# A graph network on one core: ranks and looked-up scores as maxima read from PSUM, bfloat16 masks widened by ScalarE, edge sums added in the rows' scatter

## The chip, the cores and the metric

The kernel runs on one core of one Trainium2 chip. The metric is the time of one execution on the device in microseconds (us), taken as the median over runs. Engines are called as the profile calls them: PE (TensorE matmul), PEld (its weight loads), DVE (VectorE), ACT (ScalarE), POOL (GpSimd), SP (SyncE, which issues most DMAs).

## The reference, cut to what matters

There are N = 6250 nodes with 128 features, and E = 100,000 edges sorted by their end `dst`, each with a start `src`, a weight and 128 attributes. Two graph convolutions with self-loops come first, then an attention layer over edges:

```python
h = gcn_conv(x, src, dst, ew, W1, b1)        # out[dst] += (x @ W)[src] * norm
h = gcn_conv(relu(h), src, dst, ew, W2, b2)
x = layernorm(x + sigmoid(h))
...
z, rh = x @ fc_w.T, edge_attr @ fc_r_w.T
e = leaky_relu(z[src] @ aw[0] + z[dst] @ aw[1] + rh @ aw[2])
alpha = softmax of e over the edges of one dst
agg = segment_sum(alpha[:, None] * (z[src] + rh), dst)
out = layernorm(x + relu(agg + z @ loop_w))
```

## The kernel before, in words

**Tiles.** Nodes lie in 49 blocks of 128. Edges are worked on in 49 chunks of 2048 (`NC`, `CC`), as 128 partitions by 16 (`TC`) or as 16 rows of 128 (`NL`). As the edges are sorted by `dst`, all ends of a chunk fall into a window of 144 nodes (`WC`). The sums over `dst` lie transposed in SBUF (features by nodes): `acc1`, `acc2`, and `sum_r` for the attributes.

**Slots.** Before conv1 can take rows by `src`, the edges of each chunk are sorted into slots by the block of their `src`: 12 groups (`GP`) of four blocks with 32 slots each hold "near" edges, 5 groups (`GS`) hold the rest, "far" edges. The sort is a plan of small steps, worked off beside conv1. For each chunk `count` builds a one-hot of the blocks, `oh`; `add_up` (L750 to L763) counts with matmuls into PSUM how many edges of the same block stand ahead of each place, and ACT casts that to `own` (L763); `take` (L766 to L774) multiplies `own` by `oh` on DVE (L769), folds it in three additions (L773) and reduces it to one rank per edge (L774). Later steps spread the edges' records (ACT `rec`, L818; DVE `put`, L266 and L825), gather them into slots by matmul (L834) and keep slot numbers (L842 to L847): `sdst` (the place in the window), `swt` (the weight), `sidx` (the far rows).

**One chunk of a convolution.** `pick` (L495) gets the rows. The near ones come from the table `hot` in SBUF (three bfloat16 parts that add up to float32) by 144 one-hot matmuls (L507) into PSUM, copied and scaled by ACT into `got` (L512). The far ones come from DRAM by five indirect DMAs on POOL (L516). Then DVE builds the float32 masks `wm`: 12 near ones of 144 columns in one instruction (L522), five far ones of 64 in another (L529). `weigh` (L546) lets ACT scale the far masks by their weights. `scatter` (L549) adds the chunk up with 17 float32 matmuls in PSUM (L553, each shows as two records), and `add_in` (L556) adds the window to `acc1` or `acc2` on DVE (L558). `scatter` of a chunk stands after `pick` of the next.

**Stages.** conv1 and conv2 run in the order in which the code is written (`manual_schedule`); conv3 and the tables are put in order by a planner. In conv1, `steps_now` says how many sort steps go beside each chunk. conv2 also computes, on DVE, the products of the edge attributes with the attention weights (`dots_of`, L938 and L939), and turns the `src` numbers of all edges into places with 16 transposes (`blks`). In conv3, for each half chunk, `starts` (L1249) looks up the score of each edge's `src`: a broadcast row of places `rk` is compared with the partition number (L1255), ACT doubles the block numbers (`blk2`, L1258), DVE builds the one-hot `ohb` of 8 by 50 (L260 in `equal_to`), 24 matmuls (L1263) give for each edge the scores at its place in all 49 blocks, and DVE multiplies by `ohb` (L1266, `sel`) and adds up (L1267). The PSUM pool of these has one buffer. After softmax, `edge_part` (L1385 to L1425) sums the weighted attributes: masks `mb` and `ms` (L1402, DVE), 32 matmuls (L1413), an ACT copy `sw` (L1418), two more matmuls (L1424) and `add_in` to `sum_r`. `out_of` (L450) multiplies `sum_r` by the attribute weights (L461), adds `sum_x` (L462), and a norm and a store end the work. The look-ups of later edge batches go beside the sums of earlier ones (`beside`), so the first 33 chunks of conv3 have them and the last 14 don't.

Every line number is that of the kernel before.

Of the kernel before, what the change touches and what calls it, by code (L numbers as in the profile page):

```python
# [19 lines left out]
P = 128  # L20
# [15 lines left out]
NOWHERE = 99.0  # L36


@with_exitstack
def gnn_kernel(ctx, tc, x, src, dst, ea, ew, W1, b1, W2, b2, fcw, fcrw, attn, loopw, out):  # L40
# [78 lines left out]
    srd = dram.tile([NC, GP * P], BF16, name="srd")  # L119
    drow = dram.tile([NC, P], BF16, name="drow")  # L120
# [12 lines left out]
    nc.vector.tensor_copy(iotab, iota_i)  # L133

# [16 lines left out]
    iotap, iotaq = iotap2[:, 0:1], iotap2[:, 1:2]  # L151

    trib = const.tile([P, P], BF16, name="trib")
    nc.vector.tensor_scalar(trib, iota[:, :P], iotap, None, op0=OP.is_gt)

# [36 lines left out]
    sdst = keep.tile([P, NC, G], BF16, name="sdst")  # L192
# [13 lines left out]
    blks = keep.tile([P, NC, NL], BF16, name="blks")  # L206
# [49 lines left out]
    def equal_to(out, of, n):  # L256

        row = iotab[:, :n].rearrange("p (h d) -> p h d", d=2)
        some = [P, of.shape[1], n // 2, 2]
        nc.vector.tensor_tensor(out.rearrange("p t (h d) -> p t h d", d=2), row[:, None].to_broadcast(some),  # L260
                                of[:, :, None, :].to_broadcast(some), op=OP.is_equal)
# [190 lines left out]
    def out_of(sum_x, sum_r, b0, n, xp, pool, tag):  # L452
# [6 lines left out]
        for b, nb in some:  # L459
            of = slice(b * P, b * P + nb)  # L460
            nc.tensor.matmul(agg[:nb, b - b0, :], sum_r[:, of], wfrT, start=True, stop=False)  # L461
            nc.tensor.matmul(agg[:nb, b - b0, :], sum_x[:, of], ident, start=False, stop=True)  # L462
# [35 lines left out]
    def pick(c, mask, hot, table, ps_g, wp, gots=4, fars=12):  # L498
# [15 lines left out]
        for g in range(GS):  # L514
# [5 lines left out]
        wm = wp.tile([P, GP * WC + FARS], F32, name="wm")  # L520
        parts_, at = [], 0
        nc.vector.tensor_tensor(wm[:, : GP * WC].rearrange("p (g w) -> p g w", w=WC),  # L522
                                iota[:, None, 1 : WC + 1].to_broadcast([P, GP, WC]),
                                sdst[:, c, :GP, None].to_broadcast([P, GP, WC]), op=OP.is_equal)
        for g in range(GP):
            parts_.append((0, wm[:, g * WC : g * WC + WC]))
        at = GP * WC
        if c < CF:
            nc.vector.tensor_tensor(wm[:, at:].rearrange("p (g w) -> p g w", w=FW), fiota,  # L529
                                    sdst[:, c, GP:, None].to_broadcast([P, GS, FW]), op=OP.is_equal)  # L530
        for g, (n0, w) in enumerate(far_parts[c]):
            m = wm[:, at : at + w]
            if c >= CF:
                nc.vector.tensor_tensor(m, iota[:, 1 + n0 : 1 + n0 + w],
                                        sdst[:, c, GP + g : GP + g + 1].to_broadcast([P, w]), op=OP.is_equal)
            parts_.append((n0, m))
            at += w
        wm = parts_
        return c, rows, wm

    def weigh(held):

        c, rows, wm = held
        for g in range(GP, G):
            m = wm[g][1]
            nc.scalar.activation(m, m, AF.Copy, scale=swt[:, c, g : g + 1])  # L546

    def scatter(held, ps_w):
        c, rows, wm = held  # L549
        ps = ps_w.tile([P, WC], F32, name="win")  # L550
        for g in range(G):
            n0, m = wm[g]
            nc.tensor.matmul(ps[:, n0 : n0 + m.shape[-1]], rows[g], m, start=g == 0, stop=g == G - 1)  # L553
# [7 lines left out]
    relc = ed.tile([P, NC, TC], F32, name="relc")  # L561
# [7 lines left out]
    with tc.tile_pool(name="prep", bufs=1) as prep, tc.tile_pool(name="ps_p", bufs=3, space=PSUM) as ps_mm, \  # L569
# [50 lines left out]
        nc.vector.tensor_copy(bb, bb_ps)  # L620

# [102 lines left out]
    def plan_batch(at, c0, n):  # L724
# [24 lines left out]
        def add_up(c):  # L749
# [3 lines left out]
            for h in range(2):  # L753
                ks = slice(h * HB, h * HB + HB)
                full = ps[:, h, : HB * TC].rearrange("p (k t) -> p k t", t=TC)
                nc.tensor.matmul(full, trib, oh[:, ks, :], start=True, stop=False)
# [5 lines left out]
            own = sp.tile([P, BP, TC], BF16, name="own", bufs=2)  # L762
            nc.scalar.copy(own.rearrange("p (h k) t -> p h (k t)", h=2), ps[:, :, : HB * TC])  # L763
            of["own", c] = own, oh

        def take(c):  # L766

            own, oh = of.pop(("own", c))
            nc.vector.tensor_mul(own, own, oh)  # L769
            k = BP  # L770
            while k % 2 == 0 and k > 6:
                k //= 2
                nc.vector.tensor_tensor(own[:, :k, :], own[:, :k, :], own[:, k : 2 * k, :], op=OP.add)  # L773
            nc.vector.tensor_reduce(of["r"][:, c - c0, :], own[:, :k, :].rearrange("p k t -> p t k"), AX.X, OP.add)  # L774

        def spill():
# [3 lines left out]
            nc.vector.tensor_scalar(o, of["r"], float(CAP), None, op0=OP.is_ge)  # L780
# [14 lines left out]
        def slots_of_edges():  # L795
# [9 lines left out]
            nc.vector.tensor_add(r_, r_, sub[:, some, :])  # L805
# [31 lines left out]
        def keep_slots():  # L837
# [5 lines left out]
            nc.vector.tensor_copy(sdst[:, some, :], field[:, :, 1])  # L843
# [35 lines left out]
    for c0, n in sorts:  # L879
        at = plan_batch(at if len(ends_at) != 1 else ends_at[0], c0, n)  # L880
# [90 lines left out]
    with tc.tile_pool(name="conv", bufs=2) as wp, tc.tile_pool(name="ps_g", bufs=3, space=PSUM) as ps_g, \  # L971
# [16 lines left out]
        pace = [float(done[0])]  # L988

        def steps_now(c):  # L990

            due = [(ends_at[b], max(c0 - 3 - c, 0)) for b, (c0, n) in enumerate(sorts) if ends_at[b] > pace[0]]
            pace[0] += max(((end - pace[0]) / (left + 1) for end, left in due), default=0)
            return min(int(pace[0] + 0.999), len(plan))

        held, win = None, None
        with tc.manual_schedule():
# [3 lines left out]
            for c in range(NC):  # L1001
                to = steps_now(c)
                if held is not None:
                    weigh(held)
                if win is not None:
                    add_in(acc1, c - 2, win)
                sort_to(done[0] + (to - done[0]) // 3)
                new = pick(c, mask, hot, g1, ps_g, wp, 6, 11)
# [10 lines left out]
            weigh(held)  # L1019
# [624 lines left out]
```

## Time and profile before

| | |
|---|---|
| median of 14 runs | 2257.41 us (2242.03 to 2285.51) |
| the profiled execution | 2253.38 us |
| its span, first to last instruction | 2251.3 us |
| granted TensorE clock, mean | 0.864 |
| busy: PE, PEld | 1741.4 us (77%), 1498.2 us (67%) |
| busy: DVE, ACT, POOL | 1566.3 us (70%), 996.3 us (44%), 1025.7 us (46%) |
| DMA | 306.92 MB, mean 136 GB/s |

Busy time is the time in which an engine executes; matmuls are pipelined, so a busy PE is not one at its peak. In the rows of groups, the line and engine come first, then the operation with its output and inputs, the shapes, the count after x, the total busy us and the mean ns of one, and last the engine's idle time just before these instructions with what ended it. The stages of the span, in us: preparation, degrees and the first table to 213; conv1 with the sorting to 706; the rest of conv1 to 806; the second table to 892; conv2 to 1396; the start of conv3 to 1525; conv3 with look-ups to 2047, without to 2231; the last output.

### The profile page before, as it was taken

To read this page: it belongs to the slowest core of one execution; us is meant where nothing else is said; L and a number is where in the kernel's file an instruction comes from. 1 tells how busy PE (TensorE), PEld (TensorE's weight loads), DVE (VectorE), ACT (ScalarE), POOL (GpSimd) and SP (SyncE) were. 2 spreads that over 40 slices of the span, in tenths; PEclk is the share of its full clock that TensorE was granted. 3 is DMA by queue.
4 is the path that set the end of the run, shared out by engine and by line. 5 is a ranking of instruction groups with operands and counts; after the bars stand their busy time and mean duration, and the time that the engine had idled before them with its cause. 6 is when DMAs were issued, how large, how long until landed. Compare 5 with 4: busy or idle time off the path is not lost.

```text
span 2251.3 us, 79000 instructions
## 1 busy us (share of the span) xinstructions
PE 1741.4 (77%) x33767; PEld 1498.2 (67%) x33767; DVE 1566.3 (70%) x3222; ACT 996.3 (44%) x3341; POOL 1025.7 (46%) x952
## 2 busy tenths in 40 slices
PE   2866778887788887788888887468888888888886
PEld 2545666676677765677676776357777777777775
DVE  6777766776666768866766766687777676776553
ACT  1253434443344554556565665224343343434443
POOL 4033334443335746756666764213344333434552
PEclk9886878888889975988899898568899898989998
DMA  2122222323224765665655656554656456565562
GB/s 51 38 78 68 79 81 76 92 82 89 74 78 118 249 188 165 185 165 170 192 168 174 197 171 198 166 142 125 176 152 178 135 156 170 151 167 139 147 160 62
DMA packets 261376, 306.92 MB, mean 136 GB/s; under 512 B 38387, under 2 KB 193785, under 8 KB 260212
## 3 DMA queue, kind: packets, MB, share of 16 engines
q1 hardware_dynamic: 229311, 244.90, 35.5%
q0 software_dynamic: 23520, 48.22, 10.1%
q10 hardware_dynamic: 8184, 8.65, 1.3%
q8 instruction: 268, 4.39, 0.8%
q14 instruction: 93, 0.76, 0.1%
HBM read 260.42 MB, written 41.25 MB: 134 GB/s over the span
## 4 chain that ended last, share of the span: by engine, by line
PE 64%; issue 13%; DVE 11%; ACT 5%; DMA 4%; another core or an unknown queue 3%; SPq 0%; DVEq 0%; POOL 0%; ACTq 0%; POOLq 0%
PE win L553 25%; PE g L507 20%; PE r L1413 3%; PE k L1263 2%; PE rec L834 2%; PE mm L357 2%; PE rec L1424 2%; PE r L760 1%; ACT got L512 1%; DMA rk<-srow 1%; DVE sel L1266 1%; DVE put L266 1%; PE rec L1381 1%; DVE ohm L260 1%
## 5 line engine op out<-in xcount | busy, mean ns | idle before, releaser
L516 POOL DMA_INDIRECT far<-g,sidx x490 | 640.0, 1306 | 521.4 <-PE win L553 395.7
L507 PE MATMUL g<-hot,mask 128*32 128x128 bf16 x21168 | 557.0, 245 | 260.6 <-issue 237.6
L512 ACT ACTIVATE got<-g,swt 128x128 f32<-128x128 f32 x1764 | 490.8, 377 | 476.7 <-PE g L507 235.0
L507 PEld LDWEIGHTS <-mask 128*32 128x32 bf16 x21168 | 415.1, 109 | 381.0 <-issue 355.3
L516 POOL DMA_INDIRECT far<-zd,sidx x245 | 318.3, 1299 | 506.5 <-PE win L553 410.5
L553 PE MATMUL win<-wm,got 128*128 128x144 f32 x3528 | 517.7, 306 | 6.4 <-issue 4.3
L553 PEld LDWEIGHTS win<-wm,got 128*128 128x128 f32 x3528 | 489.4, 206 | 24.5 <-issue 16.0
L522 DVE TENSOR_TENSOR wm<-iota,sdst 128x1728 f32<-128x1728 f32 x147 | 286.8, 1951 | 2.0 <-PE g L507 2.0
L546 ACT ACTIVATE wm<-wm,swt 128x64 f32<-128x64 f32 (+1 forms) x735 | 196.5, 350 | 73.8 <-DVE swt L1382 47.8
L553 PE MATMUL win<-wm,far 128*128 128x64 f32 (+1 forms) x1470 | 180.7, 269 | 2.4 <-DMA far<-g,sidx 2.3
L553 PEld LDWEIGHTS win<-wm,far 128*128 128x128 f32 x1470 | 177.9, 192 | 2.8 <-issue 2.7
L558 DVE TENSOR_TENSOR acc<-acc,win 128x144 f32 x147 | 44.5, 303 | 175.7 <-PE win L553 163.4
L1263 PE MATMUL k<-adp,rk 128*128 128x49 bf16 x2352 | 102.9, 195 | 56.2 <-DVE sel L1266 25.0
L1263 PEld LDWEIGHTS <-rk 128*128 128x128 bf16 x2352 | 87.5, 103 | 74.0 <-issue 56.3
L260 DVE TENSOR_TENSOR ohm<-iotab,pm 128x2048 bf16<-128x2048 bf16 x98 | 120.0, 1225 | 0.0
L346 POOL TENSOR_TENSOR hot<-low,hot 128x512 bf16<-128x512 f32 x24 | 38.6, 1607 | 133.8 <-DVE spilled L798 69.6
L266 DVE TENSOR_TENSOR put<-ohg,rec 128x1440 bf16<-128x1440 bf16 x49 | 45.6, 930 | 62.7 <-ACT rec L818 41.4
L763 ACT CAST own<-r 128x768 bf16<-128x768 f32 x49 | 39.5, 806 | 111.0 <-PE r L760 57.2
L1266 DVE TENSOR_TENSOR sel<-k,ohb 128x392 f32<-128x392 f32 x98 | 54.6, 557 | 47.2 <-remote 26.4
L939 DVE TENSOR_REDUCE dots<-et 128x12 f32<-128x1536 f32 (+1 forms) x49 | 85.9, 1753 | 1.6
L938 DVE TENSOR_TENSOR et<-et,ar_row 128x1536 f32<-128x1536 f32 (+1 forms) x49 | 85.5, 1745 | 0.0
L834 PE MATMUL rec<-put,ohm 128*128 128x95 bf16 x784 | 53.6, 233 | 27.7 <-DVE put L825 20.6
(401 smaller groups left out, 2275.6 us busy)
## 6 DMA issues: line engine op xcount, KB each, us to landing
et<-in_edge_attr_dram SPq DMA_DIRECT2D x97, 512.0 KB
mask<-masks SPq DMA_DIRECT2D x98, 384.0 KB
et<-in_edge_attr_dram SPq DMA_DIRECT2D x48, 768.0 KB
rk<-srow SPq DMA_DIRECT2D x98, 256.0 KB
mask<-srd SPq DMA_DIRECT2D x49, 384.0 KB
masks<-mask SPq DMA_DIRECT2D x49, 384.0 KB
ee<-in_edge_attr_dram SPq DMA_DIRECT2D x24, 512.0 KB
far<-g,sidx POOLq DMA_INDIRECT x490
```

Source lines behind the costliest of these rows:

```text
L260: nc.vector.tensor_tensor(out.rearrange("p t (h d) -> p t h d", d=2), row[:, None].to_broadcast(some), of[:, :, None, :].to_broadcast(some ...
L507: nc.tensor.matmul(ps[32 * q : 32 * q + 32, g, :], mask[:, (g0 + g) * P + 32 * q : (g0 + g) * P + 32 * q + 32], hot[:, 4 * (g0 + g) + q, k ...
L512: nc.scalar.activation(got[:, g, :], ps[:, g, :], AF.Copy, scale=swt[:, c, g0 + g : g0 + g + 1])
L516: nc.gpsimd.indirect_dma_start(out=got, out_offset=None, in_=table[:, :], in_offset=bass.IndirectOffsetOnAxis(ap=sidx[:, c, g : g + 1], ax ...
L522: nc.vector.tensor_tensor(wm[:, : GP * WC].rearrange("p (g w) -> p g w", w=WC), iota[:, None, 1 : WC + 1].to_broadcast([P, GP, WC]), sdst[ ...
L546: nc.scalar.activation(m, m, AF.Copy, scale=swt[:, c, g : g + 1])
L553: nc.tensor.matmul(ps[:, n0 : n0 + m.shape[-1]], rows[g], m, start=g == 0, stop=g == G - 1)
L834: nc.tensor.matmul(ps, ohm[:, t, :], put[:, t, :NF], start=t == 0, stop=t == TC - 1)
L938: nc.vector.tensor_mul(part, part, ar_row[:p, None, None, :].to_broadcast([p, *part.shape[1:]]))
L939: nc.vector.tensor_reduce(dots[:p, c : c + m, ts], part, AX.X, OP.add)
L1263: nc.tensor.matmul(ps[:, s, :], mk[:, s * P : (s + 1) * P], adp[:, 0, k, :NB], start=k == 0, stop=k == 2)
L1266: nc.vector.tensor_mul(sel, ps, ohb[:, :, :NB])
```

## The change

Five things are done at once.

1. *Ranks.* The triangular matrix of the counting matmul gets 4096 (`RB`) on its diagonal, so that an edge's own block holds the greatest of its 48 sums. `take` is one DVE maximum straight from PSUM; later thresholds and sums take 4096 off again. The cast, the product and the additions go.
2. *Looked-up scores.* A fourth matmul in each place adds `other`: 0 in the block of the edge and minus a great number in the other ones, from a second broadcast row `bk` of the block numbers, compared once a chunk. One DVE maximum from PSUM gives the score. `blk2`, `ohb` and `sel` go, and conv2's transposes into `blks` give way to a cast and a DMA to `bsrc`.
3. *Masks.* `sdst` is kept twice over, so that DVE compares bfloat16 pairs into `wb`; ACT copies the near masks to float32 in two halves, and scales the far ones to float32 as `weigh` did, now inside `pick`. conv2 keeps its near masks as they were (`halved=False`).
4. *Edge sums.* ACT copies the window of `edge_part` to `sr`, and the next `scatter` has it as an 18th matmul with the attribute weights. `sum_r`, its clearing on POOL, its `add_in` and L461 go. The product `ms` is made on POOL.
5. *Order.* The second batch of the sort may start four steps earlier, steps are paced in whole numbers, conv1 takes `pick` before `add_in`, masks are loaded two chunks ahead (three buffers), and the last output groups are worked off side by side.

```diff
+    iotar = const.tile([P, 1], F32, name="iotar")
+    nc.vector.tensor_scalar(iotar, iotap, 64.0, -64.0, op0=OP.is_ge, op1=OP.mult)
+    nc.vector.tensor_add(iotar, iotar, iotap)
+    other = const.tile([P, 2, NB], BF16, name="other")
+    for h in range(2):
+        nc.vector.tensor_scalar(other[:, h, :], iota[:, :NB], iotar, -BIG, op0=OP.not_equal, op1=OP.mult)
+        nc.vector.memset(other[64 - 64 * h : 128 - 64 * h, h, :], 0.0)
...
+    nc.vector.scalar_tensor_tensor(tribig, ident, RB, trib, op0=OP.mult, op1=OP.add)
...
-    sdst = keep.tile([P, NC, G], BF16, name="sdst")
+    sdst = keep.tile([P, NC, G, 2], BF16, name="sdst")
...
-            nc.tensor.matmul(agg[:nb, b - b0, :], sum_r[:, of], wfrT, start=True, stop=False)
-            nc.tensor.matmul(agg[:nb, b - b0, :], sum_x[:, of], ident, start=False, stop=True)
+            if sum_r is not None:
+                nc.tensor.matmul(agg[:nb, b - b0, :], sum_r[:, of], wfrT, start=True, stop=False)
+            nc.tensor.matmul(agg[:nb, b - b0, :], sum_x[:, of], ident, start=sum_r is None, stop=True)
...
-        wm = wp.tile([P, GP * WC + FARS], F32, name="wm")
+        wm = wp.tile([P, NEAR + FARS], F32, name="wm")
+        wb = wp.tile([P, NEAR * halved + FARS], BF16, name="wb", bufs=1)
+        if halved:
+            equal_to(wb[:, :NEAR].rearrange("p (g w) -> p g w", w=WC), sdst[:, c, :GP], WC, iota1)
+            half = GP // 2 * WC
+            for n0 in (0, half):
+                nc.scalar.copy(wm[:, n0 : n0 + half], wb[:, n0 : n0 + half])
+        else:
...
         for g, (n0, w) in enumerate(far_parts[c]):
...
+            nc.scalar.activation(m, b, AF.Copy, scale=swt[:, c, GP + g : GP + g + 1])
...
-    def weigh(held):
...
-                nc.tensor.matmul(full, trib, oh[:, ks, :], start=True, stop=False)
+                nc.tensor.matmul(full, tribig, oh[:, ks, :], start=True, stop=False)
...
-            own = sp.tile([P, BP, TC], BF16, name="own", bufs=2)
-            nc.scalar.copy(own.rearrange("p (h k) t -> p h (k t)", h=2), ps[:, :, : HB * TC])
...
-            nc.vector.tensor_mul(own, own, oh)
-            k = BP
-            while k % 2 == 0 and k > 6:
-                k //= 2
-                nc.vector.tensor_tensor(own[:, :k, :], own[:, :k, :], own[:, k : 2 * k, :], op=OP.add)
-            nc.vector.tensor_reduce(of["r"][:, c - c0, :], own[:, :k, :].rearrange("p k t -> p t k"), AX.X, OP.add)
+            nc.vector.tensor_reduce(of["r"][:, c - c0, :],
+                                    ps[:, :, : HB * TC].rearrange("p h (k t) -> p t h k", t=TC), AX.XY, OP.max)
...
-        at = plan_batch(at if len(ends_at) != 1 else ends_at[0], c0, n)
+        at = plan_batch(at, c0, n)
...
-                if held is not None:
-                    weigh(held)
+                sort_to(done[0] + (to - done[0]) // 3)
+                new = pick(c, mask, hot, g1, ps_g, wp, 6, 11)
                 if win is not None:
                     add_in(acc1, c - 2, win)
-                sort_to(done[0] + (to - done[0]) // 3)
-                new = pick(c, mask, hot, g1, ps_g, wp, 6, 11)
...
-            nc.vector.tensor_copy(d_f, s_j)
-            by_partition(ps_mm, lambda t, ps: nc.scalar.copy(blks[:, :, t], ps), lambda t: ds_[:, t, :])
+            nc.vector.tensor_copy(s_k, s_j)
+            nc.sync.dma_start(bsrc[:, :], s_k)
...
-    nc.gpsimd.memset(sum_r, 0.0)
...
+                if i % 2 == 0:
+                    bks[i // 2] = lp.tile([P, HC], BF16, name="bk", bufs=3)
+                    for h in range(2):
+                        nc.sync.dma_start(bks[i // 2][64 * h : 64 * h + 64, :],
+                                          bsrc[i // 2, None, h * HC : (h + 1) * HC].to_broadcast([64, HC]))
...
-                ohb = lp.tile([P, NL // 2, NBE], BF16, name="ohb")
-                blk2 = lp.tile([P, NL // 2, 2], BF16, name="blk2")
-                nc.scalar.copy(blk2, twice(blks[:, c, of]))
-                equal_to(ohb, blk2, NBE)
+                bk = bks[c]
+                if h == 0:
+                    nc.vector.tensor_scalar(bk, bk, iotar, None, op0=OP.is_equal)
...
+                    nc.tensor.matmul(ps[:, s, :], bk[:, s * P : (s + 1) * P], other[:, h, :], start=False, stop=True)
                 yield
-                sel = lp.tile([P, NL // 2, NB], F32, name="sel", bufs=1)
-                nc.vector.tensor_mul(sel, ps, ohb[:, :, :NB])
-                nc.vector.tensor_reduce(asr[:, 1 + c * NL + of.start : 1 + c * NL + of.stop], sel, AX.X, OP.add)
+                nc.vector.tensor_reduce(asr[:, 1 + c * NL + of.start : 1 + c * NL + of.stop], ps, AX.X, OP.max)
...
-            nc.vector.tensor_mul(ms, mb, aw[:, i, :, None].to_broadcast([P, NL, WS]))
+            nc.gpsimd.tensor_mul(ms, mb, aw[:, i, :, None].to_broadcast([P, NL, WS]))
...
-            return ps
+            sr = mp.tile([P, WC], F32, name="sr")
+            nc.scalar.copy(sr, ps)
+            return sr
...
-                    weigh(held)
                     win = scatter(held, ps_w)
-                ps = edge_part(c, aw, c - c0)
+                new[1].append(wfrT)
+                new[2].append((0, edge_part(c, aw, c - c0)))
...
-                add_in(sum_r, c, ps)
...
-        pieces.go(N, 999)
+        pieces.finish()
```

## The prediction

> **What bounds the kernel now.** I looked first at the clock of the one core (0.864 over the span), then at the chain that ended last, to see which engine sets the end.
>
> ```profile
> PE 64%; issue 13%; DVE 11%; ACT 5%; DMA 4%; another core or an unknown queue 3%; SPq 0%; DVEq 0%; POOL 0%; ACTq 0%; POOLq 0%
> ```
>
> TensorE (PE, with its issue time) is 77% of what ends last, VectorE (DVE) 11%. The change takes work mostly from DVE, so the 11% is the field in which it can win. Where it lies is read from a table of windows at the stage borders (start:end, length, busy us of PE, weight load, DVE, ACT, POOL, then clock, DMA share, GB/s):
>
> ```profile
> 213.00:706.00 493.00, 392.40 (x7257) 339.65 (x7255) 336.63 (x736) 202.75 (x708) 199.76 (x176) 0.84 0.29 82
> 706.00:806.00 100.00, 85.06 (x1988) 75.80 (x1984) 65.83 (x88) 57.61 (x206) 73.79 (x53) 0.95 0.69 211
> 892.00:1396.00 504.00, 418.90 (x8645) 365.20 (x8646) 351.44 (x442) 295.68 (x944) 331.64 (x235) 0.90 0.59 178
> 1396.00:1525.00 129.00, 72.20 (x1325) 59.93 (x1324) 95.52 (x278) 34.13 (x121) 23.43 (x17) 0.64 0.56 164
> 1525.00:2047.00 522.00, 431.78 (x9395) 383.35 (x9393) 393.68 (x969) 211.10 (x770) 205.52 (x161) 0.90 0.57 155
> 2047.00:2231.00 184.00, 150.23 (x3349) 132.38 (x3349) 97.26 (x212) 82.00 (x304) 94.80 (x69) 1.00 0.54 141
> ```
>
> They are: conv1 with the sorting, conv1's tail, conv2, the serial start of conv3, conv3 with looked-up scores (33 chunks, 15.8 us each), conv3 after them (14 chunks, about 13 us each). PE is the busiest in all but one. Only in 1396:1525 is DVE ahead (95.5 of 129 us, PE at 0.64 of its clock). In 1525:2047 DVE is near (393.7 against 431.8). Followed stage by stage, the chain gives DVE about 25 us of 493 in the first window, 43 of 129 in the fourth, 70 of 522 in the fifth: about 138 us in all. Then the rows that the change touches (form, count | busy us, mean ns | idle before and its releasers), and PE's waits in conv3 (us, times, longest):
>
> ```profile
> L522 DVE TENSOR_TENSOR wm<-iota,sdst 128x1728 f32<-128x1728 f32 x147 | 286.8, 1951 | 2.0 <-PE g L507 2.0
> L260 DVE TENSOR_TENSOR ohm<-iotab,pm 128x2048 bf16<-128x2048 bf16 x98 | 120.0, 1225 | 0.0
> L260 DVE TENSOR_TENSOR ohb<-iotab,blk 128x400 bf16<-128x400 bf16 x98 | 34.7, 355 | 0.0
> L1263 PE MATMUL k<-adp,rk 128*128 128x49 bf16 x2352 | 102.9, 195 | 56.2 <-DVE sel L1266 25.0 <-issue 20.9 <-DVE rk L1255 6.9
> L1266 DVE TENSOR_TENSOR sel<-k,ohb 128x392 f32<-128x392 f32 x98 | 54.6, 557 | 47.2 <-remote 26.4 <-PE k L1263 19.1 <-PE agg L462 1.0
> L1402 DVE TENSOR_TENSOR ms<-mb,aw 128x512 f32<-128x512 bf16 x49 | 33.4, 682 | 0.0
> L763 ACT CAST own<-r 128x768 bf16<-128x768 f32 x49 | 39.5, 806 | 111.0 <-PE r L760 57.2 <-issue 39.8 <-DVE rank L774 10.5
> L461 PE MATMUL agg<-wfrT,sum_r 128*128 128x128 f32 x96 | 22.0, 315 | 0.1
> ```
> ```profile
> PE k L1263 <- DVE sel L1266: 25.0, 22, 10.6
> PE rec L1424 <- ACT sw L1418: 21.1, 30, 1.8
> ```
>
> **The change, part by part**, on the profiled execution's own 2253.38 us (span 2251.3, 2.1 around it). That is 4.0 below the median of the 14 runs, 2257.41, so 4.0 goes on at the end.
>
> *1. Ranks.* Per chunk ACT's cast own (0.806) goes, and on DVE the product L769 (0.553), three additions L773 (0.357, 0.256, 0.206) and the reduce L774 (0.323): 1.695 us. In their place comes one maximum over 768 float32 from PSUM. No row has that; the nearest are L939 (1536 elements, 1.753; 1024, 1.213: 1.055 ns each) and L1267 (392, 0.552), which give 0.95. DVE saves 0.75 x 49 = 37 us, ACT 39.5. This lies beside PE work but for DVE's 25 of 493 us, and the ranks' waits (DVE own on ACT own, 40.6 us in 13 waits) are DVE's own idle time. The single PSUM buffer of the ranks is now freed by DVE, in whose order the maximum stands later than the cast did on ACT. I take **-5**, ends -12 and +5.
>
> *2. Looked-up scores.* PE gets 16 matmuls more per chunk (a fourth beside three), 784 in all. From the row L1263 they cost 44 ns each when busy (102.9/2352): **+34**. Ends: the fastest group of 24 took 0.77 us, 32 ns each, so +25; with the idle time of the row (159.1/2352 = 68 ns) +53. DVE loses sel (0.557) and ohb (0.355) of each half chunk and gains one bk comparison per chunk (as L1255, 0.50): -1.3 us a chunk. ACT loses 20 us of blk2. Off the chain comes what waited on sel, 25.0 us; of ohb's 34.7 busy us I count 23% (in the fourth and fifth windows 113 of DVE's 489 busy us were on the chain): -8. The 16 transposes taken out of conv2 are within 2 us. Two more DMAs a chunk go on SP's queue and, 128 KB each by their tile, are small beside 512 KB et loads; cover gone, the rk wait of 6.9 us shows their size. Sum **+1**, ends -20 and +33.
>
> *3. Masks.* By L260 (355 ns at 400, 1225 at 2048) 1728 bf16 elements in pairs take 1.06 us against 1.95, 320 take 0.31 against 0.48: DVE saves 1.06 us a chunk in conv1 and conv3, about 104 in all. ACT pays two copies of 864, 0.9 each by its slope between 512 (0.615) and 768 (0.806) plus start: 1.75 x 98 = 172 us. ACT is 41% busy in both windows, so it has room; but on its queue they and the five far scales (0.35 each) now stand right after got, ahead of rec L818 (DVE's put waited 40.6 us on it in 22 waits) and of sw L1418 (PE waited 21.1 us in 30). `wb` has one buffer: DVE's next mask waits for these copies, with puts and score maxima queued behind it, but a chunk (13 us) lies between. DVE gives time back, ACT takes it at the next hand-over: **0**, ends -10 and +40 (22 waits x 1.8 us).
>
> *4. Edge sums.* L461's 96 records go, -22.0 PE; the 18th scatter matmul adds 49 x 0.293 (two records of 147 ns at L553) = +14.4. DVE loses 49 add_in of 0.304, 14.9 us, by the same 23%: -3. The clear of sum_r (5.45 us on POOL at 1436.88) goes; beside it one rk comparison took 2.34 instead of 0.50 us: -2. ACT gets a 144-wide copy, 0.29 x 49, hidden: the scatter that needs it is the next chunk's. ms moves from DVE (0.682) to POOL, between far gathers; the 32 r matmuls wait for it, and behind them on PE stand L1424 and the next chunk's g. POOL is about 40% busy there, a 512-wide product takes it 1.15 to 2.23 (L346). Against it, DVE's 512-wide L344 went from 0.677 to 1.644 beside POOL's arithmetic: +0.97 x 49 = 47 us of DVE if every ms meets such an operation, 23% of it on the chain: +11, less 23% of the 33.4 that leave DVE: -8. Sum -22.0 + 14.4 - 3 - 2 + 11 - 8, **-10**, ends -20 and +30.
>
> The Trainium skill, "SBUF — State Buffer", section "Who interferes with whom", speaks against this move: a VectorE operation with two SBUF inputs contends with a GpSimd instruction that reads SBUF. The rows of L344 and L346 agree in kind. Taken as a full lock of one median L346 (1.456 us) per chunk it would add up to 71 us of DVE time instead of the 47, still mostly off the chain.
>
> *5. Order.* The second sort batch starts four steps earlier, conv1 adds a window after pick, masks load two ahead, and the last output groups run interleaved. After 2231 the chain has two rounds of load, norm and store (fin<-x1d alone 3.21 us at 2234.64); interleaving spares about one: -4. Mask and sort timing: -2, the size of one hot or rk wait. **-6**, ends -12 and +10.
>
> Sum: -5 + 1 + 0 - 10 - 6 = **-20**: 2253.4 - 20 = 2233.4, plus 4.0: **2237**.
>
> **Rivals.**
> *A. DVE paces more than its chain share says.* For it: 393.7 of 522 us busy, and PE's unexplained issue gaps (13%) come with a low clock, which a steadier feed would raise. Against: in conv2, with DVE at 70%, chunks of 7.6 us stand beside 14.1 ones and the chain holds no DVE. Half of the 138 DVE chain us come back (-69), 34 - 7.6 are paid on PE (+26), and 20 of the 74 us of issue gaps before g in conv1 close: 2257.4 - 69 + 26 - 20 = about 2195.
> *B. PE is the bound: slower.* The place is 1525:2047, 33 chunks. The added k matmuls stand on the bounding engine at 68 ns (less 7.6 from part 4), and the freed DVE time is idle because PE's k wait on sel becomes a wait on the maximum that reads the same single PSUM buffer, and the 25 us stay. Part 5 gives its -6, the clear -2, the rest nothing: 2257.4 + 53 - 7.6 - 6 - 2 = 2295 at the price with idle time, 2276 at 34, 2267 at 25; middle about **2280**. It decides from the point where PE's idle time in that window (90 us) falls by less than what is put on PE there, 528 matmuls x 44 ns = 23 us.
> *C. Hidden.* Gains and PE's price cancel, as they do in part 2 alone: 2250 to 2264.
> That the pairs don't run at the paired rate, so that DVE gains nothing in part 3 and ACT pays, leads to B as well.
>
> **How the numbers follow.** Forecast (2215 to 2250) 0.42; A (below 2215) 0.15; C 0.15; B (above 2264) 0.28. A difference of 0.3%, 6.8 us, is about the least that can be told from none here: faster 0.57, same 0.15, slower 0.28. The range that leaves out no more than the outer tails of A and B, and takes in the ends of parts 2 and 3 one at a time, is 2188 to 2288; the forecast's own is 2215 to 2250.
>
> **What will show it.** Ranks: one DVE reduce near 0.95 us and no ACT own. Scores: 3136 k matmuls, their busy sum near 137 us, PE's wait on sel replaced by one clearly under 25 us. Masks: a bf16 row of 1.06 us and ACT copies of 0.9 us; put's wait on rec not above 41 us. Edge sums: no L461 pair; POOL's ms between 1.15 and 2.2 us. Windows: the start of conv3 near 110 us, conv3 with scores near 15.4 us a chunk, conv1 little changed. It is wrong if conv1 slows with ACT rec or got as releaser, if a chunk of conv3 takes over 15.8, or if PE's issue gaps (36.5 us before g in conv3) move by tens of us.

## The result, and the profile after

The changed kernel takes 2431.90 us (median of 10 runs, 2419.08 to 2443.50) against 2264.99 us (47 runs): a ratio of 1.0755, 95% interval 1.0722 to 1.0788. The prediction was 2237, with 2188 to 2288 as its range. The profiled execution took 2425.22 us, its span 2423.4, its clock 0.832 (before 0.864). Its busy times are PE 1824.6 us (+83), DVE 1346.8 (-220), ACT 1114.2 (+118), POOL 965.1 (-61): DVE gave back 220 of some 250 us that the prediction's parts add up to, and the time went up.

The same stages in the changed kernel, as windows (start:end, length, PE, weight load, DVE, ACT, POOL, clock, DMA share, GB/s): conv1 with the sorting, its tail, conv2, the start of conv3, conv3 with look-ups and without.

```profile
219.00:718.00 499.00, 384.79 (x7189) 331.77 (x7189) 269.81 (x589) 229.94 (x740) 187.87 (x176) 0.85 0.29 80
718.00:856.00 138.00, 103.46 (x1842) 87.03 (x1845) 52.22 (x81) 68.97 (x204) 56.53 (x51) 0.78 0.47 147
938.00:1466.00 528.00, 427.66 (x8602) 371.64 (x8590) 350.38 (x447) 295.41 (x947) 329.97 (x238) 0.87 0.58 172
1466.00:1609.00 143.00, 84.99 (x1654) 72.86 (x1654) 84.59 (x248) 36.22 (x107) 20.25 (x21) 0.64 0.65 189
1609.00:2190.00 581.00, 457.56 (x9860) 411.14 (x9858) 298.90 (x784) 262.63 (x793) 193.87 (x192) 0.84 0.55 152
2190.00:2404.00 214.00, 170.27 (x3353) 154.32 (x3351) 71.73 (x181) 109.20 (x346) 81.86 (x83) 0.86 0.43 119
```

PE is busy for 75 to 81% of the windows but the fourth, and nobody else for more, so no engine is busy enough to be the bound by itself. Of the 172 us that the span grew, 83 are more busy time of PE and 89 more idle time. From the end of one scatter to another, the 172 us are: +13 in conv1 to its 37th chunk, +44 in the ten chunks after, -9 at the second table, +24 in conv2, +13 at the start of conv3, +59 with look-ups, +30 without; 2 us less at conv1's end. The last window has neither sort steps nor look-ups, and still loses 30 us over its 15 chunks, 2.0 us each: its clock fell from 1.00 to 0.86 and DVE's busy time from 97 to 72 us. The groups that answer to those of before (count | busy, mean ns | idle before, releasers):

```profile
L783 DVE TENSOR_REDUCE rank<-r 128x16 f32<-128x768 f32 x49 | 46.7, 953 | 89.4 <-PE r L776 89.3
L1267 PE MATMUL k<-adp,rk 128*128 128x49 bf16 x2352 | 132.5, 201 | 70.0 <-DVE asr L1270 33.5 <-issue 27.6 <-DMA rk<-srow 4.6
L1270 DVE TENSOR_REDUCE asr<-k 128x8 f32<-128x392 f32 x98 | 54.9, 561 | 28.8 <-remote 16.5 <-PE k L1268 11.9
L273 DVE TENSOR_TENSOR wb<-iota,sdst 128x1728 bf16<-128x1728 bf16 x98 | 102.9, 1050 | 88.4 <-ACT wm L559 88.4
L541 ACT CAST wm<-wb 128x864 f32<-128x864 bf16 x196 | 171.5, 934 | 29.1 <-PE win L568 26.6 <-DVE wb L273 2.5
L1406 POOL TENSOR_TENSOR ms<-mb,aw 128x512 f32<-128x512 bf16 x49 | 51.4, 1049 | 96.4 <-ACT aw L1342 50.0 <-remote 34.7 <-issue 5.8
L273 DVE TENSOR_TENSOR mb<-iotab,rel 128x512 bf16<-128x512 bf16 x49 | 20.8, 424 | 218.7 <-POOL ms L1406 218.7
L568 PE MATMUL win<-sr,wfrT 128*128 128x144 f32 x98 | 22.8, 314 | 0.0
L1428 PE MATMUL rec<-pl,sw 128*128 128x144 f32 x194 | 51.4, 405 | 61.4 <-ACT sw L1422 60.6 <-issue 0.4
```

The durations are where the prediction had them or better: 0.953 us for the maximum (0.95), 1.05 for the pairs (1.06), 0.93 for a copy (0.9), and 1.05 for ms, under its 1.15 to 2.2. What is new stands in the idle columns: DVE waits 218.7 us for ms and 88.4 us for ACT to empty wb, and in DVE's order everything behind these waits too.

**Two groups of sittings.** The kernels of one sitting run on one chip, one after the other. In some sittings the kernel before takes 2265 to 2332 us (group A, with the result above), in others 1944 to 1952 (group B). The chip numbered 6 stood in both groups, so what makes the difference stays open; each ratio here is against the kernel before of its own sitting.

### The profile page after: what moved, and what is told of

It reads as the page before. It is cut to its first block, busy times and chain, and to the rows that moved or that the text cites. A ratio compares the mean times of both kernels' runs of the same rounds, so it can differ in the third digit from the quotient of the medians.

```text
span 2423.4 us, 80127 instructions
## 1 busy us (share of the span) xinstructions
PE 1824.6 (75%) x34535; PEld 1577.9 (65%) x34535; DVE 1346.8 (56%) x2789; ACT 1114.2 (46%) x3437; POOL 965.1 (40%) x1000
## 4 chain that ended last, share of the span: by engine, by line
PE 37%; issue 6%; ACT 5%; another core or an unknown queue 5%; DMA 4%; DVE 4%; POOL 1%; SPq 0%; ACTq 0%; DVEq 0%; POOLq 0%
PE win L568 15%; PE g L521 11%; ACT wm L541 2%; PE k L1267 2%; DMA rk<-srow 2%; PE rec L1428 2%; PE rec L1385 1%; POOL far L530 1%; ACT got L526 1%; PE agg L476 1%; PE mm L370 1%; DMA far<-g,sidx 1%; PE k L1268 1%; PE mm L444 1%
## 5 line engine op out<-in xcount | busy, mean ns | idle before, releaser
L530 POOL DMA_INDIRECT far<-g,sidx x490 | 607.0, 1239 | 620.3 <-PE win L568 495.8
L521 PE MATMUL g<-hot,mask 128*32 128x128 bf16 x21168 | 575.5, 255 | 264.6 <-issue 251.9
L530 POOL DMA_INDIRECT far<-zd,sidx x245 | 244.6, 998 | 537.3 <-PE win L568 453.3
L559 ACT ACTIVATE wm<-wb,swt 128x64 f32<-128x64 bf16 (+1 forms) x735 | 195.2, 360 | 65.2 <-DVE swt L1386 50.6
L1267 PE MATMUL k<-adp,rk 128*128 128x49 bf16 x2352 | 132.5, 201 | 70.0 <-DVE asr L1270 33.5
L541 ACT CAST wm<-wb 128x864 f32<-128x864 bf16 x196 | 171.5, 934 | 29.1 <-PE win L568 26.6
L273 DVE TENSOR_TENSOR wb<-iota,sdst 128x1728 bf16<-128x1728 bf16 x98 | 102.9, 1050 | 88.4 <-ACT wm L559 88.4
L273 DVE TENSOR_TENSOR mb<-iotab,rel 128x512 bf16<-128x512 bf16 x49 | 20.8, 424 | 218.7 <-POOL ms L1406 218.7
L1268 PE MATMUL k<-other,bk 128*128 128x49 bf16 x784 | 116.8, 200 | 9.0 <-issue 9.0
L279 DVE TENSOR_TENSOR put<-ohg,rec 128x1440 bf16<-128x1440 bf16 x49 | 45.4, 927 | 105.1 <-ACT rec L828 99.2
L1428 PE MATMUL rec<-pl,sw 128*128 128x144 f32 x196 | 51.6, 403 | 61.4 <-ACT sw L1422 60.6
L783 DVE TENSOR_REDUCE rank<-r 128x16 f32<-128x768 f32 x49 | 46.7, 953 | 89.4 <-PE r L776 89.3
L543 DVE TENSOR_TENSOR wm<-iota,sdst 128x1728 f32<-128x1728 f32 x49 | 95.5, 1950 | 1.1 <-POOL hot L359 1.1
```

What stands on the lines that cost most here:

```text
L521: nc.tensor.matmul(ps[32 * q : 32 * q + 32, g, :], mask[:, (g0 + g) * P + 32 * q : (g0 + g) * P + 32 * q + 32], hot[:, 4 * (g0 + g) + q, k ...
L530: nc.gpsimd.indirect_dma_start(out=got, out_offset=None, in_=table[:, :], in_offset=bass.IndirectOffsetOnAxis(ap=sidx[:, c, g : g + 1], ax ...
L541: nc.scalar.copy(wm[:, n0 : n0 + half], wb[:, n0 : n0 + half])
L543: nc.vector.tensor_tensor(wm[:, :NEAR].rearrange("p (g w) -> p g w", w=WC), iota[:, None, 1 : WC + 1].to_broadcast([P, GP, WC]), sdst[:, c ...
L559: nc.scalar.activation(m, b, AF.Copy, scale=swt[:, c, GP + g : GP + g + 1])
L783: nc.vector.tensor_reduce(of["r"][:, c - c0, :], ps[:, :, : HB * TC].rearrange("p h (k t) -> p t h k", t=TC), AX.XY, OP.max)
```

## The experiments

**Undoing masks, scales and ms (group B).** Theory H: ScalarE's copies and scales stand in its queue ahead of what others wait for. Theory G: ms on GpSimd holds conv3 up. Theory P: PE is the bound and pays for the added matmuls. All runs start from the changed kernel.

```diff
masks_f32
-    def pick(c, mask, hot, table, ps_g, wp, gots=4, fars=12, halved=True):
+    def pick(c, mask, hot, table, ps_g, wp, gots=4, fars=12, halved=False):
ms_vector
-            nc.gpsimd.tensor_mul(ms, mb, aw[:, i, :, None].to_broadcast([P, NL, WS]))
+            nc.vector.tensor_mul(ms, mb, aw[:, i, :, None].to_broadcast([P, NL, WS]))
weigh_late (the same loop, where weigh stood before; fb, two buffers, holds the far masks)
-            nc.scalar.activation(m, b, AF.Copy, scale=swt[:, c, GP + g : GP + g + 1])
+            scales.append((m, b, swt[:, c, GP + g : GP + g + 1]))
...
+        for m, b, s in pending.pop(held[0]):
+            nc.scalar.activation(m, b, AF.Copy, scale=s)
```

> The changed kernel with the near masks written as float32 by VectorE in all three layers, as conv2 has them; all else as changed. Theory H (hand-over: ScalarE's copies and scales stand in its queue ahead of what the others wait for) expects conv1's +55 us and a good part of conv3's +89 us back: about 2320 to 2340 us. Theory P (TensorE is the bound and pays for the 784 added matmuls) expects within 15 us of the changed 2432. Theory G (the ms product on GpSimd holds up conv3) expects only conv1's part back, about 2380.

> The changed kernel with the far masks' scales moved back to where they stood before (one chunk later, just ahead of the scatter), near masks still in pairs and copied by ScalarE. Theory H with the scales at fault expects conv2's +24 us back and half of the rest: about 2340 to 2370. If the near copies are at fault: 2400 to 2410, conv2's part alone. Theories P and G: within 15 us of 2432.

> The changed kernel with the product ms on VectorE again. Theory G expects conv3's +1.9 us a chunk back, 2340 to 2360. Theories H and P expect 2415 to 2435.

> Both undone: float32 near masks by VectorE and ms on VectorE. H and G together expect the sum of the two single steps, about 2280 to 2300, with conv2's +24 left. P expects still over 2400.

| run | us | of before (1951.58) | interval |
|---|---|---|---|
| masks_f32 | 2058.41 | 1.0577 | 1.0537 to 1.0616 |
| weigh_late | 2008.51 | 1.0315 | 1.0278 to 1.0352 |
| ms_vector | 1979.09 | 1.0175 | 1.0133 to 1.0217 |
| masks_f32_ms_vector | 1955.70 | 1.0038 | 1.0014 to 1.0062 |

The expected times were for the level of group A, so only the ratios can be held against them, and the changed kernel itself was never timed in group B. Two differences need no control. With float32 masks, bringing ms back to VectorE takes 1.0577 to 1.0038, 103 us. In the two traces, whose spans lie 77 us apart, all of it is in conv3 (from the second scatter to the last 744 us against 663). With ms on VectorE, float32 masks take 1.0175 to 1.0038, 23 us. So in this group G names the larger part, H a small one, and P, which wanted the last run well over before, falls. How ms costs 103 us when it takes 1.05 us on a half idle engine, the waits of masks_f32 say (DVE, then POOL, then PE; us, times, longest), beside PE's with ms back:

```profile
DVE mb L273 <- POOL ms L1406: 159.6, 44, 4.4
```
```profile
POOL far L530 <- PE win L568: 548.7, 185, 17.2
```
```profile
PE k L1267 <- DVE asr L1270: 86.9, 35, 4.8
```
```profile
PE k L1267 <- DVE asr L1270: 39.8, 42, 3.7
```

POOL's queue holds the far gathers, which wait for the scatter to free their buffers. ms stands among them; mb has one buffer, so DVE's next mb waits for ms; the score maxima stand behind mb on DVE; and PE's k waits for them. The 103 us are shown; that they arise by this chain is read from the waits.

**The same steps in group A, with the control.**

> The changed kernel as it is, as a control: the four runs before ran on a chip on which the kernel before takes 1952 us, not 2265. If the loss is the same work on any chip, about 1.075 of the kernel before. From the single steps (masks_f32 1.058, weigh_late 1.032, ms_vector 1.018), all of which undo part of it, it has to be over 1.058 if each of them helps.

> The kernel before as it is, for its trace on this chip: conv3 with and without look-ups chunk by chunk, to set beside the runs with one step undone. Expected near 1950 us if it is the same chip.

> Changed kernel with the product ms on VectorE and the far scales back in their old place; the near masks still in pairs and copied by ScalarE. Theory G (ms on GpSimd is the main cause): about 1.01, as ms_vector, less what the scales cost. Theory H (ScalarE's queue): clearly below ms_vector's 1.018, about 0.995.

> Float32 near masks by VectorE, far scales in the old place, ms on VectorE: of the change only ranks, looked-up scores, edge sums and order are left. Theories G and H: 0.985 to 1.00, since then only what the prediction had as gains is left. Theory P (the added matmuls and the maximum from PSUM cost): 1.00 to 1.02.

| run | us | of before (2332.20) | interval |
|---|---|---|---|
| changed_again | 2460.51 | 1.0588 | 1.0497 to 1.0678 |
| weigh_late_ms_vector | 2523.14 | 1.0850 | 1.0748 to 1.0951 |
| masks_scales_ms_back | 2359.57 | 1.0140 | 1.0047 to 1.0233 |

(before_again, a single run, took 2325.19 us.) Here the order is another. With scales and ms back the kernel is slower still, by 63 us, against both G and H as I had put them; why is open. The last two runs differ by the near masks alone, in pairs through ACT or in float32 by DVE: 164 us, 7% of before, where group B showed 1.4% (there with the scales inside pick). So the pairs are the main loss in group A, and something that group B has not makes them so dear.

**Leaving the gathers out.** PE's largest wait in group A is "issue" ahead of the g matmuls. In the trace it is a crawl: four to six matmuls, 0.45 us of nothing, again and again, while POOL's far gathers run. Theory S: beside these gathers PE can't issue short matmuls at its rate.

```diff
-            got = wp.tile([P, D], F32, name="far", bufs=fars)
-            nc.gpsimd.indirect_dma_start(
-                out=got, out_offset=None, in_=table[:, :],
-                in_offset=bass.IndirectOffsetOnAxis(ap=sidx[:, c, g : g + 1], axis=0))
-            rows.append(got)
+            rows.append(nofar)
```

`nofar` is one tile of zeros, so the kernel leaves the far edges out of all sums; every matmul, mask and copy stays.

> The changed kernel without the 735 far gathers: the far rows are one tile of zeros, so the far edges are left out of all three layers' sums; every matmul, mask and copy stays. Theory S (on the chips where the kernel before takes over 2250 us, PE issues only some 13 instructions per us while GpSimd's gathers run undisturbed, and the pairs leave them undisturbed): PE's stalls ahead of the g matmuls fall from 267 to 299 us to under 60, and the time by 250 us or more below the changed kernel's 1.06 to 1.075 of before. Theory H (ScalarE's queue) expects the stalls to stay, as they would be PE's own.

> As no_gathers: the changed kernel without the 735 far gathers, the far edges left out of the sums. On a chip with the stalls theory S expects them to fall from 267 to 299 us to under 60 and the time below 0.92 of before; if the stalls are PE's own, they stay over 200 us and the time over 1.0. On a chip without them: 0.973 again.

> The changed kernel once more, as a control on this call's chip. On a chip without the stalls (before near 1950 us): over masks_f32's 1.058 if both undone steps help alone, or between 1.03 and 1.06 if float32 masks make ms on GpSimd dearer. On a chip with them: 1.06 to 1.075, as twice before.

> The kernel before, for its trace on this chip: chunk times of conv1, of conv3 with and without look-ups. Near 1950 or near 2300 us, by the chip.

no_gathers met group B: 1893.15 us, 0.9729 of before (0.9658 to 0.9800). no_gathers_2 met group A: 1891.76 us, 0.8301 (0.8253 to 0.8349), beside changed_2 with 2436.28, 1.0692 (1.0629 to 1.0755), and before_2 with 2283.08 in a single run. Without gathers the two groups are the same to 1.4 us; in group A they cost the changed kernel 2436 - 1892 = 544 us. PE's waits of before_2, changed_2 and no_gathers_2, from one sitting:

```profile
PE g L507 <- issue: 233.5, 511, 2.8
```
```profile
PE g L521 <- issue: 260.2, 510, 2.7
```
```profile
PE g L523 <- issue: 44.7, 29, 4.5
```

That the crawl belongs to the gathers is shown; S holds so far. The g matmuls alone account for 421 of the 544 us: their busy time fell from 574.5 to 369.4 us, the issue time before them from 260.2 to 44.7. The granted clock rose with it, from 0.831 (changed_2) to 0.915.

Why do pairs make it worse, when the gathers are the same? Look at the start of a chunk in the tail of conv1, before (start, us, engine, line, operation):

```profile
764.50 0.94 POOL L516 DMA_INDIRECT far<-g,sidx  x1 [2.11 <-PE win L553]
765.05 1.01 PE L507 MATMUL g<-hot,mask 128*32 128x128 bf16 x42
765.38 1.95 DVE L522 TENSOR_TENSOR wm<-iota,sdst 128x1728 f32<-128x1728 f32 x1
765.74 2.64 POOL L516 DMA_INDIRECT far<-g,sidx  x1 [0.30 <-issue]
766.54 1.98 PE L507 MATMUL g<-hot,mask 128*32 128x128 bf16 x102 [0.48 <-issue]
```

and in the changed kernel:

```profile
799.47 1.06 DVE L273 TENSOR_TENSOR wb<-iota,sdst 128x1728 bf16<-128x1728 bf16 x1 [8.46 <-ACT wm L559]
800.26 1.09 POOL L530 DMA_INDIRECT far<-g,sidx  x1 [7.06 <-PE win L568]
800.80 1.05 PE L521 MATMUL g<-hot,mask 128*32 128x128 bf16 x46
...
801.65 0.94 POOL L530 DMA_INDIRECT far<-g,sidx  x1 [0.30 <-issue]
...
802.31 0.29 PE L521 MATMUL g<-hot,mask 128*32 128x128 bf16 x5 [0.45 <-issue]
...
802.89 0.94 POOL L530 DMA_INDIRECT far<-g,sidx  x1 [0.30 <-issue]
...
803.06 0.26 PE L521 MATMUL g<-hot,mask 128*32 128x128 bf16 x4 [0.47 <-issue]
803.79 0.29 PE L521 MATMUL g<-hot,mask 128*32 128x128 bf16 x6 [0.47 <-issue]
...
804.14 0.94 POOL L530 DMA_INDIRECT far<-g,sidx  x1 [0.30 <-issue]
...
804.54 0.26 PE L521 MATMUL g<-hot,mask 128*32 128x128 bf16 x4 [0.45 <-issue]
...
805.39 0.94 POOL L530 DMA_INDIRECT far<-g,sidx  x1 [0.30 <-issue]
...
807.38 2.22 PE L521 MATMUL g<-hot,mask 128*32 128x128 bf16 x74 [1.10 <-issue]
807.53 3.30 ACT L526 ACTIVATE got<-g,swt 128x128 f32<-128x128 f32 x12 [8.10 <-remote]
```

Before, DVE's float32 mask starts just after the scatter, when the gathers' buffers come free; the gather beside it takes 2.64 us instead of 0.94, and 102 g matmuls start in that time. In the changed kernel the mask is done early and short: five gathers run one after the other, each 0.94 to 1.09 us, and PE crawls from 801.9 to 807.4, until 1 us after the last. ACT's copies come after that, wb is freed after them, and so DVE's next mask comes early and short again. Over whole kernels of group A, the gathers of under 1.0 us grow with the loss: 430 of 735 before (433 in before_again), 457 in masks_scales_ms_back (1.014), 480 and 483 in the changed kernel (1.06 and 1.075), 532 in weigh_late_ms_vector (1.085). lookups_back and changed_2 fit in with 442 (1.0037) and 475 (1.069). In group B the count tells nothing: far_first has 533 at 1.036. Over whole traces, where gathers meet g matmuls, PE starts 27 of these a us during gathers of under 1.1 us and 42 during those of over 1.8 in the kernel before, 16 and 30 in the changed one. Over all gathers it is 33 against 24; the rates of before with the changed kernel's mix of lengths would give 32. So having fewer long gathers explains little of the loss by itself.

Nor does the reading reach conv3, where 89 of the 172 us are; it fits the tail of conv1. PE's waits in the tail before and changed, then in conv3 with look-ups before and changed:

```profile
PE g L507 <- issue: 12.4, 29, 1.4
```
```profile
PE g L521 <- issue: 34.1, 74, 1.1
```
```profile
PE g L507 <- issue: 35.7, 90, 0.6
```
```profile
PE g L521 <- issue: 23.1, 42, 1.6
```

Over the whole kernel the issue time before g grew by only 14 us (251.9 against 237.6). PE's busy time is up 83 us: 35 for k, 22 for rec, 19 for g and 14 for the scatters with their 18th matmul, less 6 each for agg and r. In conv3 PE waits more for ACT's sw instead, 60.6 us against 27.0. ACT itself was idle for 47 of the 61 us, so this is no backlog of mask copies in its queue, as theory H would have it; what holds sw up is not shown. Between the two runs that differ by the masks alone it is the same: 100 of the 151 us between their traces are in conv3, the wait for sw is 86.8 us against 37.1, and the issue time before g 295.4 against 261.7.

The Trainium skill, "SBUF — State Buffer", "Who interferes with whom", has a VectorE operation with two SBUF inputs contend with a GpSimd instruction that reads SBUF. L522 has two such inputs, and the gather beside it took 2.64 us; gathers with no two-input VectorE operation beside them took 0.96 us on average in that trace, those beside L522 1.92. That is as the rule has it if a gather counts as such a reader of SBUF, which no run here shows.

**Moving the gathers, and putting the mask back.** The far matmuls second to sixth in a scatter free the gathers' buffers some 3 us earlier, and masks_twice lets DVE write the float32 masks again ahead of the pairs, with nothing taken away.

```diff
far_first (far_first_before has the same order in the kernel before)
+        pairs = list(zip(rows, wm))
+        pairs = pairs[:1] + pairs[GP:G] + pairs[1:GP] + pairs[G:]
-        for g, (row, (n0, m)) in enumerate(zip(rows, wm)):
+        for g, (row, (n0, m)) in enumerate(pairs):
masks_twice
+            nc.vector.tensor_tensor(wm[:, :NEAR].rearrange("p (g w) -> p g w", w=WC),
+                                    iota[:, None, 1 : WC + 1].to_broadcast([P, GP, WC]),
+                                    sdst[:, c, :GP, 0:1].to_broadcast([P, GP, WC]), op=OP.is_equal)
```

> The changed kernel, with the five far matmuls of each scatter placed second to sixth instead of last. Their buffers come free some 3 us earlier, so the next gathers run beside the scatter (68 instructions in 4 to 5 us) instead of beside the 288 of the g matmuls. Theory S: stalls ahead of g down by half or more, 2300 to 2350 where the changed kernel takes 2430 to 2460. Theory H: no change, within 15 us.

> The kernel before with the same reordering of the scatter. Theory S: 60 to 150 us faster than before on a chip with the stalls (250 to 285 us of them), and less than for the changed kernel, as its gathers are already stretched by VectorE's float32 masks. If the order of the scatter itself is what counts: the same gain in both.

> Float32 near masks, late scales and ms on VectorE (1.014 of before without this), with the far matmuls early. Theory S: below far_first_before if ranks, looked-up scores and edge sums bring what they were meant to: 0.93 to 0.97 of before. If they cost (theory P): 1 to 2% above far_first_before.

> The changed kernel with more work: ahead of the pairs VectorE also writes the near masks in float32 into wm, as before, and ScalarE writes the same values over them; 98 x 1.95 = 191 us more for VectorE, nothing taken away. On a chip with the stalls, theory S with shielding (VectorE's float32 masks hold up the gathers, and PE runs meanwhile) expects it faster than the changed kernel: 1.02 to 1.05 of before instead of 1.06 to 1.075. Theory H (ScalarE's copies and the hand-over to them cost) expects 1.07 to 1.10. On a chip without the stalls: no control there, some 1.03 to 1.08.

> The kernel before with the far matmuls second to sixth in each scatter, as far_first_before, which was 1.023 on a chip without the stalls. On a chip with them theory S expects 0.94 to 0.98, since the gathers then run beside the scatter. If 1.02 again, the order of the scatter costs more than the collision with g.

All five met group B, so they don't decide what they were made for. far_first_before is 1.0228 of before in both sittings (1991.23 and 1992.98 us; 1.0174 to 1.0282, 1.0184 to 1.0273): without the crawl the other order of the scatter costs 2%, so it is no safe change to make. far_first is 1.0362 (2018.52 us), far_first_masks_back 1.0195 (1993.51). masks_twice is 1.0722 (1.0681 to 1.0763; 2090.57 us): in group B, where the changed kernel has no time to set beside it, nothing shows that DVE's extra work helps. What stays open is whether in group A the stretched gathers are the cause of the part in g, as the timeline suggests, or go with it, and what the pairs cost in conv3.

**The look-ups.** masks_scales_ms_back with the look-ups in the old form (`blks`, `ohb`, `sel`; the fourth matmul and bk out); ranks, edge sums and order stay changed.

```diff
-                    nc.tensor.matmul(ps[:, s, :], bk[:, s * P : (s + 1) * P], other[:, h, :], start=False, stop=True)
...
-                nc.vector.tensor_reduce(asr[:, 1 + c * NL + of.start : 1 + c * NL + of.stop], ps, AX.X, OP.max)
+                sel = lp.tile([P, NL // 2, NB], F32, name="sel", bufs=1)
+                nc.vector.tensor_mul(sel, ps, ohb[:, :, :NB])
+                nc.vector.tensor_reduce(asr[:, 1 + c * NL + of.start : 1 + c * NL + of.stop], sel, AX.X, OP.add)
```

> As masks_scales_ms_back (float32 near masks, late scales and ms on VectorE), with the looked-up scores in the old form too: no fourth matmul, ohb and sel on VectorE, transposes in conv2. Left of the change are ranks, edge sums and order. Theory P (the 784 added matmuls cost more than what VectorE gives back): conv3 with look-ups falls by 20 to 35 us against masks_scales_ms_back, the time to 0.985 to 1.00 of before. If the look-ups pay for themselves, as predicted (+1 us): 1.01 to 1.015 on a chip with stalls, 1.00 to 1.005 on one without.

Group A: 2279.09 us, 1.0037 (0.9995 to 1.0079), against 1.0140 (1.0047 to 1.0233) with the new look-ups in another sitting. The two intervals overlap. Each beside its own kernel before, one trace each, conv3 with look-ups is +21 us with the new form and +7 with the old: some 14 us of price, if that is more than the spread between sittings. It is less than the 20 to 35 that P wanted, more than my +1. What is left of the change in lookups_back, ranks, edge sums and order, stands so beside before_2 of its sitting: conv1 to the 37th chunk 695 against 713 us, its tail 109 against 98, conv2 518 against 529, conv3 with look-ups 529 against 521, without 202 against 189. The gain in conv1 is not firm: masks_scales_ms_back has the same conv1 and stands at 711 against 707, its tail at 122 against 103; conv2 (540 against 548) and the last stage (207 against 196) agree. No run that does all the work beats the kernel before.

## Why the prediction was wrong

*What bounds the kernel.* "TensorE is 77% of what ends last" was the frame, and it was kept too simple. 13% of the span in that view was issue time, set from outside. I named these gaps unexplained and let them stand as a constant. no_gathers_2 shows that most of those before g belong to the gathers (260.2 us with them, 44.7 without), so a change that moves the gathers can move them.

*Part 1, ranks: the size right, the gain not settled.* The maximum took 0.953 us and the cast went. conv1 to its 37th chunk is 18 us shorter in lookups_back and 4 us longer in masks_scales_ms_back, with the order's part in both, where I had -5 and -2. DVE now waits 89.3 us for PE's counts, in its own idle time.

*Part 2, look-ups: +34 of PE busy time was right* (k went from 102.9 to 137.6 us as the union of its records). What failed is "off the chain comes what waited on sel, 25.0 us": PE waits 33.5 us on the maximum, which reads the same single PSUM buffer. That was rival B's mechanism. The price is some 14 us instead of +1, one trace each.

*Part 3, masks: the step that failed most.* It was priced at 0, ends -10 and +40, and measured 164 us in group A (1.0850 against 1.0140), 23 in group B (1.0175 against 1.0038). The overlap that it relied on, "but a chunk (13 us) lies between", did not hold: DVE stood idle for 88.4 us in 22 waits until ACT had emptied wb. I counted VectorE's shorter mask as time given back, and never asked what the long mask had been holding up. The order in ACT's queue did happen too: DVE's put waits 99.2 us on rec where I had set 41 as the mark. How the 164 us come about is open: the crawl fits the tail of conv1, and for conv3 the record shows only where PE waits.

*The scales inside pick.* I had no price for them apart from the masks. conv2, whose near masks are unchanged, went up 24, 12 and 7 us in the three traced pairs. In before_again's sitting it took 561 us in changed_again, and 544 and 540 in the two runs with late scales. Neither the near masks nor ms differ in conv2, so the scales cost some 17 to 20 us there, by one trace each. For the rest of the kernel no run undid them alone in group A, and weigh_late's 1.0315 in group B has no control.

*Part 4, edge sums and ms.* Two errors. L461 was costed by its busy sum (22.0) and the added matmul by its spacing (14.4); by one measure, 96 records of 315 ns went and 98 of 314 came. Overlaps counted once, agg fell from 29.1 to 23.0 us and the scatters rose from 701.9 to 716.4, so the sum should have had +8 and not -7.6. And ms was priced as contention on ports (+11) when what it met was a queue: mb's single buffer, DVE waiting 218.7 us. In group B that is 103 us; in group A it can't be told apart from the crawl, as weigh_late_ms_vector shows. The last window, without look-ups, is still 13 us up in lookups_back and 11 in masks_scales_ms_back; there only the edge sums and the order are left, so together they cost.

*Part 5, order.* After the last PE instruction come 15.4 us (15.2 before): interleaving gained nothing of its -4.

*The rivals.* B had the right sign and a part of the mechanism, the wait on the maximum. But what it added was the k matmuls, 25 to 53 us, of which 35 us of busy time came; it gave the masks and ms nothing, and those were the larger part. No rival had a shorter instruction on one engine cost time on two others.

## What to carry to other kernels

Before shortening an instruction on an engine that isn't the bound, list what runs beside it and what it delays: its length may be what keeps two others apart, as the tail of conv1 suggests here without proving it. For an instruction moved to another engine, price its place in that queue and the buffers of its inputs, and who stands behind whoever fills them, not its duration. And cost what goes and what comes by one measure, busy sum or spacing, never by both.

## What the runs showed of the hardware

In some sittings PE issued 128x32 by 128x128 bf16 matmuls at four to six per 0.72 us beside GpSimd's indirect gathers. In the changed kernel's trace they started 42 ns apart on average during a gather and up to 1.1 us after it, and 21 ns apart elsewhere (pauses over 0.8 us left out). In group B it was 15 ns beside gathers (masks_f32_ms_vector), as without any (no_gathers). PE had some 500 issue gaps before these matmuls, mostly of about 0.45 us, against 29 to 54 in group B. The kernel before took 2270.37 us in a sitting with them and 1950.46 in one without. The scatter's float32 matmuls, 147 ns a record, overlap with gathers for 381 us in the changed kernel's trace and have 3.3 us of issue gaps in all. Without gathers the changed kernel took 1893.15 and 1891.76 us in the two groups. No run tells why one sitting has it and another not.
